# A state space layer inside a four-layer block: the fourth tap of its convolution moves to VectorE, the taps stay in SBUF, the diagonals are made over more turns, and the decays get a fourth slot

## The chip, the core and the metric

The kernel runs on one core of one Trainium2 chip. The metric is the device time of one execution in microseconds (us). Five engines work side by side, each through its own queue in order: TensorE (PE, with its weight loads PEld), VectorE (DVE), ScalarE (ACT), GpSimd (POOL) and SyncE (SP), which here issues almost all DMAs. An instruction that waits holds up all that stands behind it on its engine.

## What is computed

The input x holds 8 sequences of 512 positions with 256 channels. Three transformer layers come first; the change does not touch them. The fourth layer is a bidirectional state space (Mamba) layer with an MLP, conditioned by per-sequence scales and shifts. Its core, per direction:

```python
xz = h @ in_proj_W                       # 256 -> 1024
x, z = jnp.split(xz, 2, axis=-1)         # 512 channels each
xc = conv over time of x, 4 taps per channel, causal
x = silu(xc + conv_b)
xdbl = x @ x_proj_W                      # 512 -> 16 + 32 + 32
dt = softplus(xdbl[..., :16] @ dt_proj_W + dt_proj_b)
def step(hst, inp):                      # state: 512 channels x 32
    dA = exp(dt_t[:, :, None] * A)
    hst = hst * dA + dt_t[:, :, None] * B_t[:, None, :] * x_t[:, :, None]
    y = einsum('bdn,bn->bd', hst, C_t)
...
y = ys + Dp * x
return y * silu(z) @ out_proj_W
```

The forward and the backward direction are added, then `x + g1 * (fwd + bwd)`, a second norm and `silu(h @ w1) * (h @ w2) @ w3` follow. All is fp32.

## The kernel before, in words

**Shape of the fourth layer.** It takes the time from about 3455 us to the end. The work is 16 *passes*: for each of the 8 sequences b a forward pass, then a backward one (even numbers 0, 2, ... 14 are forward, odd ones backward). A pass (`recur`, L1145) is a loop of 64 *turns* k. A turn takes 32 channels with 8 of the 32 states each (128 partitions times two tiles of 512 positions). This text counts in *pairs* of turns, p = 0 to 31 in each pass, since the kernel issues them by twos. One pair is, on the engines:

- PE: 64 small matmuls that spread dt·B·x over the partitions into two PSUM tiles `bx` (`fill`, L1166). `bx` has three buffers, so the fill of a turn waits for the scans three turns back. The moving side of the fills are diagonal matrices `dg` made from B.
- ACT: four exponentials `da` (`decay`, L1179) into slots `da_t`, three of them, one for each turn in rotation: the decay of a turn waits for the scans three turns back. `da` is made from `dtr`, dt spread by DMA over the partitions (`spread`, L1110).
- DVE: four `tensor_tensor_scan` (L1190), one per tile, that run the recurrence; the output goes into one of four `hs` tiles (one for each pair). The order is scans of the first turn, then those of the second, and small DVE work is issued between the two.
- POOL: one product of the pair's `hs` with C (`cs`, L1194).

Every second pair PE adds up 8 matmuls over `hs` into `yc` (`sums`, L1222); they stand two pairs behind the POOL product that they read. Behind the last sum of a quarter pass (16 turns), `take` (L1203 on DVE backward, L1205 on ACT forward) moves `yc` to `ys`.

**The work around the recurrence** is issued between the turns by two Python generators, so the order on every queue is written out by hand (`manual_schedule`). At each even turn, after the pair's fills and decays, the main loop (L1313 to L1326) takes up to two pieces of each stream, `prep` and `post`, as long as a credit for PE work lasts. A piece says its cost by what it yields; a yield of LAST or more ends that stream's part of this turn.

- `prep` of the next pass (`before`, `prep3`): for a forward pass norm, `w_x0` product into `xp` (L950), convolution, SiLU of `u` (L959), products with `w_x` and `w_dt`, softplus, `uc` on POOL (L1006), transposes into `ut`. For a backward pass the same `xp` is convolved in the other direction (`convolve(b, True)`), and the gates `zs` are made (L912).
- `post` of the sequence before (`behind`): `project` (L1045) and `mlp3` (L1052).

All their products go through one PSUM tile `bank`, which has one buffer: the next product starts only after the last one was read. So backward passes carry the forward `prep` of the next sequence: norm at pairs 0 to 5, `xp` at pairs 6 and 7, convolution at pairs 8 to 13, SiLU at 14. Forward passes carry the backward convolution at pairs 0 to 3 and 8, `project` at 4 and 5, gates at 9 to 11 with SiLU, then both the projections of dt and the MLP.

**Convolution** (`convolve`, L916). Per group of 128 channels PE multiplies four diagonal tap matrices with four shifted views of `xp` (L929: four fp32 matmuls of 128x128 by 512, two records each in the trace), ACT adds the bias and writes `u` (L934), and SiLU follows later (L959). The 16 diagonal matrices are built once on DVE (L830), written to DRAM (`conv_s`) and read back in two halves before every convolution, through the ring `order` with `use` (L801) and `fetch` (L787), which has two buffers shared with `w_x0` and `w_z0`.

**Diagonals** (`diagonal`, L1124). For each of the four gp of the next pass there are four parts s: three on ACT (8 small activations each, L1133), one on POOL (L1137). They are due 1, 2, 3 and 4 turns after the fills of the last quarter have used the old ones (L1249).

**Decays of the next pass.** `spread` for the first `dtr` tile of the next pass is issued in turn 61, those for the next three at the head of the pass (L1151), behind the `cs` loads in SP's queue.

Of the kernel before, what the change touches and what calls it, by code (L numbers as in the profile page):

```python
# [25 lines left out]
N_U, N_UT, N_UC, N_DT, N_HS = 7, 5, 1, 5, 4  # L26
PAIRED = True
SUMS_LATE, DIAG, STAGGER, RATE, CREDIT = 3, "AAPA", 2, 4.0, 4.0
# [45 lines left out]
def dit_mamba_kernel(ctx: ExitStack, tc: tile.TileContext, t, out):  # L74
    nc = tc.nc
# [695 lines left out]
    with ExitStack() as mctx:  # L771
# [8 lines left out]

        conv_s = [scr.tile([128, 8, 128], F32, tag=f"cv{i}", name="conv_s", bufs=1) for i in range(2)]
        order = ["w_x0", "cv0", "cv1"]
        for b in range(B):
            order += ["cv0", "cv1", "w_z0"] + ["w_x0", "cv0", "cv1"] * (b + 1 < B)
        ring = {}

        def fetch(name, tag="wp", bufs=2):  # L787
            w = mp_.tile([128, 1024], F32, tag=tag, name="w", bufs=bufs)
            if name in ("w_x0", "w_z0"):
                src, k = t["w_in"].rearrange("(k p) m -> p k m", p=128), 2  # L790
                src = src[:, :, 0:D_IN] if name == "w_x0" else src[:, :, D_IN:]
            elif name[:2] == "cv":
                src, k = conv_s[int(name[2])], 8
            else:
                k = t[name].shape[0] // 128
                src = t[name].rearrange("(k p) m -> p k m", p=128)
            m = src.shape[-1]
            ring[name] = w[:, 0 : k * m].rearrange("p (k m) -> p k m", k=k)
            nc.sync.dma_start(ring[name], src)

        def use(name):  # L801

            assert order.pop(0) == name
            if order:
                fetch(order[0])
            return ring[name]

# [18 lines left out]

        for i in range(2):
            w = mp_.tile([128, 8, 128], F32, tag="wp", name="conv_d", bufs=2)
            for j in range(8):
                nc.vector.tensor_scalar(w[:, j, :], ident, vcol("convw", 8 * i + j), None, ALU.mult)  # L830
            nc.sync.dma_start(conv_s[i], w)
        dp_d = mp_.tile([128, 4, 128], F32, tag="dp_d", name="dp_d")
        for c in range(4):
            nc.vector.tensor_scalar(dp_d[:, c, :], ident, vcol("Dp", c), None, ALU.mult)

        da_t = [mp_.tile([128, 2, L], F32, tag=f"da{i}", name="da") for i in range(3)]
        xp = mp_.tile([128, 4, L + 6], F32, tag="xp", name="xp")
# [4 lines left out]

        WAIT, LAST = -1, 100
        st = {}
# [60 lines left out]
        def gates(b):  # L905
            h = st.pop(("hz", b))
            zs = mp_.tile([128, 4, L], F32, tag="zs", name="zs")
            st["zs", b] = zs
            w = use("w_z0")
            for c in range(4):  # L910
                p = yield from dense(w, h, 2, c)
                nc.scalar.copy(zs[:, c, :], p)  # L912
                taken()
                yield 2

        def convolve(b, rev):  # L916
            us = st["us"] = []
            for c in range(4):
                if c % 2 == 0:
                    w = use(f"cv{c // 2}")  # L920
                while n_u[0] - n_u[1] >= N_U:
                    yield WAIT
                n_u[0] += 1
                p = yield from free_bank()
                for k in range(4):
                    if k == 2:
                        yield 2
                    o = 6 - k if rev else k
                    nc.tensor.matmul(  # L929
                        p, w[:, (c % 2) * 4 + k, :], xp[:, c, o : o + L],  # L930
                        start=k == 0, stop=k == 3,
                    )
                us.append(mp_.tile([128, L], F32, tag="u", name="u", bufs=N_U))
                nc.scalar.activation(us[c], p, AF.Identity, bias=vcol("convb", c))  # L934
                taken()
                yield 2

        def prep3(b, rev):

            if not rev:  # L940
                h = st["hz", b]

                r = mp_.tile([128, L], F32, tag="uc", name="rstd", bufs=N_UC)
                yield from norm3(
                    h, h, xp[:, 0:2, 3 : L + 3], r, col(sc3[0], 0, b), col(sh3[0], 0, b)
                )
                w = use("w_x0")
                for c in range(4):
                    p = yield from dense(w, h, 2, c)
                    nc.scalar.copy(xp[:, c, 3 : L + 3], p)  # L950
                    taken()
                    yield 2
                yield from convolve(b, rev)
            us = st.pop("us")
            if rev:
                zs = st["zs", b]
                nc.scalar.activation(zs, zs, AF.Silu)
            for u in us:
                nc.scalar.activation(u, u, AF.Silu)  # L959
            use_exp_ln(pin=False)  # L960
            yield LAST
            p = yield from free_bank()
# [35 lines left out]
            use_exp_ln(pin=False)  # L998
            yield LAST
            nc.sync.dma_start(dt_s.rearrange("(c p) t -> p c t", p=128), dt)  # L1000
            st["dt", b, rev] = True

            def transposed(c):

                uc = mp_.tile([128, 4, 2, 64], F32, tag="uc", name="uc", bufs=N_UC)
                nc.gpsimd.tensor_tensor(uc, halves(us[c]), halves(dt[:, c, :]), ALU.mult)  # L1006
                yield 0
                yield 0
                while n_ut[0] - n_ut[1] >= N_UT:
# [41 lines left out]

        def mlp3(b):  # L1052
            x = st.pop(("x", b))
            fetch("w_g1", "wq", 1)
            h = mp_.tile([128, 2, L], F32, tag="h", name="h")
            g = mp_.tile([128, 3, L], F32, tag="g3", name="g3")
# [8 lines left out]
            use_exp_ln(pin=False)  # L1065
            yield LAST
            yield LAST
            for c in range(3):
                p = yield from dense(ring["w_g2"], h, 2, c)
                yield 2 + LAST  # L1070
                nc.vector.tensor_tensor(g[:, c, :], g[:, c, :], p, ALU.mult)
                taken()
            fetch("w_g3", "wq", 1)
            yield LAST
# [67 lines left out]

        n_pairs, done, projected, credit = [0], set(), set(), [0.0]

        def recur(step, nxt, ys):  # L1145
# [9 lines left out]

            hs, yc, bx, da_of = {}, {}, {}, {}

# [14 lines left out]

            def decay(k):
                c, gp, j = k // 16, k % 16 // 4, k % 4
                da = da_of[k] = da_t[n_pairs[0] % 3]
                n_pairs[0] += 1
                for i in range(2):
                    g = 2 * gp + i
                    nc.scalar.activation(  # L1179
                        da[:, i, :], dtr[step, 4 * c + j], AF.Exp, scale=negA[:, 4 * c + j, g : g + 1]  # L1180
                    )

            def scan(k):
                t_, j = divmod(k, 2)
                if j == 0:
                    hs[t_] = mp_.tile([128, 2, 2, L], F32, tag="hs", name="hs", bufs=N_HS)
                da, x = da_of.pop(k), bx.pop(k).rearrange("p r (t i) -> p i (r t)", i=2)
                for i in range(2):
# [10 lines left out]
            def take(c):  # L1199

                assert rev or b == 0 or b - 1 in projected
                if rev:
# [28 lines left out]
            for k in range(n_k):  # L1231
                c, gp, j = k // 16, k % 16 // 4, k % 4
                run_due(1)
                if PAIRED:
                    if k % 2 == 0:
                        fill(k)
                        fill(k + 1)
                        decay(k)
                        decay(k + 1)
                else:  # L1240
                    fill(k)
                    decay(k)
                n_ut[1] += k % 16 == 15
                later(2, lambda k=k: scan(k))
                if j == 3:
                    later(2 + SUMS_LATE, lambda c=c, gp=gp: sums(c, gp))
                    if c == 3 and nxt:
                        for s in range(4):
                            later(1 + s, lambda gp=gp, s=s: diagonal(nxt, gp, s))  # L1249
                        later(4, lambda gp=gp: spread_c(nxt, gp))  # L1250
                if c < 3:
                    if k % 16 in (6, 13, 14, 15):
                        spread(step, 4 * (c + 1) + (6, 13, 14, 15).index(k % 16))
                elif k % 16 == 13 and nxt and ("dt",) + nxt in st:
                    spread(nxt, 0)
                yield k
# [28 lines left out]
        def behind(b, ys):  # L1285
# [3 lines left out]
            yield from project(b, ys)  # L1289
            yield from mlp3(b)  # L1290
            if b + 1 < B:
# [13 lines left out]
        for i, step in enumerate(steps):  # L1305
# [7 lines left out]
            for k in recur(step, nxt, ys):  # L1313


                if k % 2 == 0 or not PAIRED:
                    credit[0] = min(credit[0] + (RATE if PAIRED else RATE / 2), CREDIT)
                    first = b and not rev and b - 1 not in projected
                    for stream in (post, prep) if first else (prep, post):
                        for _ in range(2):  # L1320
                            cost = next(stream, WAIT) if credit[0] > 0 else WAIT
# [3 lines left out]
                            if cost >= LAST:  # L1325
                                break  # L1326
            for _ in prep:
                pass
# [112 lines left out]
```

## Time and profile before

| quantity | value |
|---|---|
| median of 3 runs | 6533.63 us (6531.69 to 6535.91) |
| the profiled execution | 6532.14 us |
| its span, first to last instruction | 6530.3 us |
| first scan of the fourth layer | 3564.6 us |
| last scan ends | 6459.6 us |
| pass 0, pass 1 | 177.1, 175.9 us |
| forward passes 2 to 14 | 188.6 to 192.4 us |
| backward passes 3 to 13 | 176.3 to 178.5 us |
| pass 15, with nothing to prepare | 145.2 us |

Pass lengths are counted from the scans in the timeline, 128 to a pass, from first scan to first scan. In the profile a group is a line of the kernel with an engine, its busy time, the mean of one instruction, and the idle time of that engine ahead of it with what ended it. Two activations on ACT overlap a little, so four decays take 2.45 us although one shows 0.71; four scans on DVE take 4.47 us although one shows 1.20. The granted clock of PE was 0.96 of full speed on average.

### The profile page before, as it was taken

What the parts mean: (1) busy time and instruction counts of PE and PEld (TensorE: products, weight loads), DVE (VectorE), ACT (ScalarE), POOL (GpSimd) and SP (SyncE); (2) the same over time, 40 slices, a digit from 0 to 9 for tenths busy, and PEclk for the clock granted to TensorE, in tenths of its full rate; (3) what the DMA queues carried; (4) which work ended last, traced back from release to release, by engine and by line L of the source; (5) the groups of instructions that cost most, each with busy time, mean ns of one, the idle gap of its engine ahead of it and who ended that gap; (6) DMA issues with size and microseconds to landing.
All of it is one profiled execution on the core that took longest, in us unless ns stands there. A gap on an engine that the chain in (4) does not pass through costs nothing.

```text
span 6530.3 us, 200997 instructions
## 1 busy us (share of the span) xinstructions
PE 5907.6 (90%) x89056; PEld 2936.4 (45%) x89056; DVE 4073.5 (62%) x5042; ACT 3552.8 (54%) x6919; POOL 3664.6 (56%) x1464
## 2 busy tenths in 40 slices
PE   8999999999999989999986889888888889888887
PEld 4333345555555553333332444444444444444443
DVE  4555545454555445444521887878888887878886
ACT  2444444333343333444434776777777776777773
POOL 1010126565556662111101888888888888888896
PEclk8999999999999999999997999999999999999999
DMA  2101100100000000101002111222221212222120
GB/s 85 26 22 28 32 31 27 33 17 27 27 17 26 27 17 26 42 21 29 20 11 71 58 46 57 68 61 62 60 69 57 71 42 61 68 59 63 55 63 24
DMA packets 173457, 278.16 MB, mean 43 GB/s; under 512 B 40993, under 2 KB 58913, under 8 KB 172593
## 3 DMA queue, kind: packets, MB, share of 16 engines
q1 hardware_dynamic: 172048, 264.27, 13.8%
q8 instruction: 703, 11.52, 0.8%
q14 instruction: 162, 1.32, 0.1%
q10 hardware_dynamic: 544, 1.05, 0.0%
HBM read 203.30 MB, written 35.65 MB: 37 GB/s over the span
## 4 chain that ended last, share of the span: by engine, by line
PE 66%; POOL 12%; ACT 10%; issue 6%; DVE 4%; SPq 1%; DMA 1%; POOLq 0%; DVEq 0%; ACTq 0%
PE s L380 10%; PE s L673 8%; POOL hs L1194 8%; PE bx L1166 7%; PE s L636 5%; PE s L586 4%; PE bank L859 4%; PE yc L1222 4%; PE bank L929 4%; PE o L606 3%; PE s L497 3%; ACT da L1179 3%; PE o L537 3%; PE s L527 3%; DVE hs L1190 2%
## 5 line engine op out<-in xcount | busy, mean ns | idle before, releaser
L1190 DVE TENSOR_TENSOR_SCAN hs<-da,bx 128x512 f32<-128x512 f32 x2048 | 2310.2, 1199 | 542.1 <-ACT da L1179 347.9
L1194 POOL TENSOR_TENSOR hs<-hs,cs 128x2048 f32<-128x2048 f32 x512 | 2322.7, 4563 | 347.6 <-DVE hs L1190 242.1
L1179 ACT ACTIVATE da<-dtr,negA 128x512 f32<-128x512 f32 x2048 | 1342.9, 714 | 284.4 <-DVE hs L1190 246.4
L1166 PE MATMUL bx<-dg,ut 64*32 64x128 f32 x65536 | 1125.6, 276 | 252.3 <-DVE hs L1190 158.7
L1166 PEld LDWEIGHTS bx<-dg,ut 64*32 64x32 f32 x65536 | 940.8, 107 | 652.7 <-issue 469.2
L518 POOL TENSOR_SCALAR pr<-pr,sums 128x512 f32<-128x512 f32 x512 | 796.8, 1575 | 572.1 <-DVE sums L516 560.1
L591 DVE TENSOR_REDUCE negp<-s 128x1 f32<-128x512 f32 x1024 | 637.5, 683 | 586.3 <-PE s L586 586.0
L642 ACT ACTIVATE pt<-s 128x512 f32<-128x512 f32 x1024 | 528.0, 601 | 440.9 <-PE s L636 440.8
L1222 PE MATMUL yc<-hs,r 128*32 128x512 f32 x4096 | 614.8, 634 | 71.1 <-POOL hs L1194 70.9
L509 ACT ACTIVATE pr<-s,negm 128x512 f32<-128x512 f32 x512 | 345.1, 686 | 298.4 <-DVE negm L508 284.9
L528 DVE COPY pt<-s 128x512 f32<-128x512 f32 x512 | 322.0, 683 | 193.8 <-PE s L527 179.6
L508 DVE TENSOR_REDUCE negm<-s 128x1 f32<-128x512 f32 x512 | 317.3, 682 | 142.1 <-PE s L497 142.0
L586 PE MATMUL s<-kT,qT 32*128 32x512 f32 x2048 | 366.7, 651 | 35.9 <-ACT pt L642 18.2
L673 PE MATMUL s<-g,w_w 128*128 128x512 f32 x768 | 365.4, 623 | 23.9 <-ACT g L737 14.6
L1133 ACT ACTIVATE dg<-eye,bt 128x64 f32<-128x64 f32 x1536 | 381.5, 345 | 0.0
L352 POOL TENSOR_TENSOR xs<-x 128x512 f32<-128x512 f32 x48 | 61.0, 1271 | 566.1 <-DVE x L662 187.2
L380 PE MATMUL s<-h,w_w 128*128 128x512 f32 x768 | 364.1, 615 | 12.2 <-POOL h L371 12.2
L380 PE MATMUL s<-h,wqkv 128*128 128x512 f32 x768 | 365.9, 611 | 5.1 <-POOL h L371 5.1
L636 PE MATMUL s<-q,kT 32*128 32x512 f32 x2048 | 364.8, 647 | 2.4 <-DVE qs L453 1.9
L699 POOL COPY wide<-rec 128x1024 f32<-128x1024 f32 x16 | 16.6, 1037 | 622.3 <-DVE rec L697 622.3
L1222 PEld LDWEIGHTS yc<-hs,r 128*32 128x32 f32 x4096 | 126.3, 112 | 463.0 <-issue 292.1
L527 PE MATMUL s<-base,pr 128*128 128x128 f32 x2048 | 266.2, 281 | 43.0 <-POOL pr L518 38.5
(168 smaller groups left out, 6336.3 us busy)
## 6 DMA issues: line engine op xcount, KB each, us to landing
dtr<-dt_s SPq DMA_DIRECT2D x1024, 64.0 KB
cs<-c_s SPq DMA_DIRECT2D x256, 128.0 KB
wqkv<-in_wqkv_dram SPq DMA_DIRECT2D x48, 512.0 KB
w<-conv_s SPq DMA_DIRECT2D x32, 512.0 KB
dt_s<-dt SPq DMA_DIRECT2D x16, 1024.0 KB
x_mid<-x SPq DMA_DIRECT2D x24, 512.0 KB
x<-x_mid SPq DMA_DIRECT2D x24, 512.0 KB
w<-in_w_g_dram SPq DMA_DIRECT2D x24, 384.0 KB
```

Of the source, the lines that this page charges most:

```text
L380: nc.tensor.matmul(p, w[:, k, o : o + 128], src[:, k, :], start=k == 0, stop=k == n - 1)
L518: nc.gpsimd.tensor_scalar(p[:, j, :], p[:, j, :], sums[:, j : j + 1], None, ALU.mult)
L586: nc.tensor.matmul(ss[j], u.qT[r, c, qt * 128 : (qt + 1) * 128], u.kT[r, c, :], start=True, stop=True)
L591: nc.vector.tensor_reduce(negp[c % 2][:, qt, i : i + 1], ss[j], AX.X, ALU.max, negate=True)
L636: nc.tensor.matmul(ss[j], u.kT[r, c, i * 128 : (i + 1) * 128], q2[u, c][r, :], start=True, stop=True)
L642: nc.scalar.activation(pt[j // 2][:, j % 2, :], ss[j], AF.Exp)
L673: nc.tensor.matmul(p, w[:, first + c, m * 128 : (m + 1) * 128], srcs[c], start=c == 0, stop=c == n - 1)
L1166: nc.tensor.matmul(bx[k][32 * n : 32 * n + 32, r, 128 * s : 128 * s + 128], uts[c][64 * r : 64 * r + 64, s, 32 * j : 32 * j + 32], d[64 * ...
L1179: nc.scalar.activation(da[:, i, :], dtr[step, 4 * c + j], AF.Exp, scale=negA[:, 4 * c + j, g : g + 1])
L1190: nc.vector.tensor_tensor_scan(h, back(da[:, i, :]), back(x[:, i, :]), 0.0, ALU.mult, ALU.add)
L1194: nc.gpsimd.tensor_tensor(hs[t_], hs[t_], cs[step, k % 16 // 4][:, None, :, :].to_broadcast([128, 2, 2, L]), ALU.mult,)
L1222: nc.tensor.matmul(yc[c][32 * j : 32 * j + 32, :], r32, h[j // 2][:, j % 2, i, :], start=False, stop=gp == n_p - 1 and i == 1, tile_positi ...
```

## The change

- **Convolution.** PE does three taps. The fourth reads `xp` without a shift in both directions; DVE multiplies it with its weight and adds PSUM in one `scalar_tensor_tensor` that writes `u`. The activation with the bias on ACT goes; the bias moves into the SiLU. The piece ends its stream's part of the turn, so the DVE instruction is issued one even turn after its matmuls, between the two halves of that pair's scans on DVE.
- **Taps.** 12 diagonal matrices stay in SBUF. The trip through DRAM and the 32 loads go. The ring keeps `w_x0` and `w_z0` alone, with one buffer; the next is fetched after the last product that uses it (`used`).
- **Diagonals.** The four parts are due 1, 4, 7 and 10 turns after, in place of 1, 2, 3 and 4; the part on POOL moves by four turns.
- **Decays.** Four slots in place of three; `decay` moves out of `recur` unchanged (AHEAD is 0, so each pair's decays are issued where they were). The first four `dtr` tiles of the next pass are issued in turns 54, 61, 62 and 63.
- **MLP.** Its `h` takes the second half of `ys` in place of a tile of its own.
- **Turns.** After a change of ACT's table a piece yields ALONE, which also ends the turn for the other stream. The listing of the built program shows what this does in a forward pass: the square of the MLP's norm is issued at pair 8 in place of 11, behind the SiLU; the scale and shift of its `h` at pair 17 in place of 16, behind softplus; its six first matmuls at pairs 18 and 19 in place of 17 and 18.

```diff
-PAIRED = True
+N_DA, AHEAD, SPREAD = 4, 0, (6, 13, 14, 15)
...
-        conv_s = [scr.tile([128, 8, 128], F32, tag=f"cv{i}", name="conv_s", bufs=1) for i in range(2)]
-        order = ["w_x0", "cv0", "cv1"]
+        order = ["w_x0"]
         for b in range(B):
-            order += ["cv0", "cv1", "w_z0"] + ["w_x0", "cv0", "cv1"] * (b + 1 < B)
+            order += ["w_z0"] + ["w_x0"] * (b + 1 < B)
...
-        for i in range(2):
-            w = mp_.tile([128, 8, 128], F32, tag="wp", name="conv_d", bufs=2)
-            for j in range(8):
-                nc.vector.tensor_scalar(w[:, j, :], ident, vcol("convw", 8 * i + j), None, ALU.mult)
-            nc.sync.dma_start(conv_s[i], w)
+        conv_d = mp_.tile([128, 12, 128], F32, tag="conv_d", name="conv_d")
+        for c in range(4):
+            for k in range(3):
+                nc.vector.tensor_scalar(
+                    conv_d[:, 3 * c + k, :], ident, vcol("convw", 4 * c + k), None, ALU.mult
+                )
...
-        da_t = [mp_.tile([128, 2, L], F32, tag=f"da{i}", name="da") for i in range(3)]
+        da_t = [mp_.tile([128, 2, L], F32, tag=f"da{i}", name="da") for i in range(N_DA)]
...
-                for k in range(4):
+                for k in range(3):
                     if k == 2:
                         yield 2
                     o = 6 - k if rev else k
                     nc.tensor.matmul(
-                        p, w[:, (c % 2) * 4 + k, :], xp[:, c, o : o + L],
-                        start=k == 0, stop=k == 3,
+                        p, conv_d[:, 3 * c + k, :], xp[:, c, o : o + L],
+                        start=k == 0, stop=k == 2,
                     )
                 us.append(mp_.tile([128, L], F32, tag="u", name="u", bufs=N_U))
-                nc.scalar.activation(us[c], p, AF.Identity, bias=vcol("convb", c))
+                yield 1 + LAST
+
+                nc.vector.scalar_tensor_tensor(
+                    us[c], xp[:, c, 3 : L + 3], vcol("convw", 4 * c + 3), p, ALU.mult, ALU.add
+                )
                 taken()
-                yield 2
...
-            for u in us:
-                nc.scalar.activation(u, u, AF.Silu)
+            for c, u in enumerate(us):
+                nc.scalar.activation(u, u, AF.Silu, bias=vcol("convb", c))
             use_exp_ln(pin=False)
-            yield LAST
+            yield ALONE
...
-                            later(1 + s, lambda gp=gp, s=s: diagonal(nxt, gp, s))
+                            later(1 + 3 * s, lambda gp=gp, s=s: diagonal(nxt, gp, s))
...
-                if c < 3:
-                    if k % 16 in (6, 13, 14, 15):
-                        spread(step, 4 * (c + 1) + (6, 13, 14, 15).index(k % 16))
-                elif k % 16 == 13 and nxt and ("dt",) + nxt in st:
-                    spread(nxt, 0)
+                if k % 16 in SPREAD:
+                    i = SPREAD.index(k % 16)
+                    if c < 3:
+                        spread(step, 4 * (c + 1) + i)
+                    elif nxt and ("dt",) + nxt in st:
+                        spread(nxt, i)
...
-            yield from mlp3(b)
+            yield from mlp3(b, ys[:, 2:4, :])
...
+                        if cost >= ALONE:
+                            break
```

## The prediction

> **What bounds the kernel now.** I first read the page's shares and slices, for which stretch the change touches:
>
> ```profile
> PE 5907.6 (90%) x89056; PEld 2936.4 (45%) x89056; DVE 4073.5 (62%) x5042; ACT 3552.8 (54%) x6919; POOL 3664.6 (56%) x1464
> ...
> DVE  4555545454555445444521887878888887878886
> ACT  2444444333343333444434776777777776777773
> POOL 1010126565556662111101888888888888888896
> ```
>
> Up to slice 21 (about 3455 us) lie three layers that stay as they are. In the fourth, DVE, POOL and PE are all eight to nine tenths busy: no engine bounds all of it, so the stage decides. Next, the groups that make a pair of turns:
>
> ```profile
> L1190 DVE TENSOR_TENSOR_SCAN hs<-da,bx 128x512 f32<-128x512 f32 x2048 | 2310.2, 1199 | 542.1 <-ACT da L1179 347.9
> L1194 POOL TENSOR_TENSOR hs<-hs,cs 128x2048 f32<-128x2048 f32 x512 | 2322.7, 4563 | 347.6 <-DVE hs L1190 242.1
> L1166 PE MATMUL bx<-dg,ut 64*32 64x128 f32 x65536 | 1125.6, 276 | 252.3 <-DVE hs L1190 158.7
> ```
>
> A pair costs POOL 4.56, DVE 4.47 (from scan to scan where nothing waits), PE 1.96 for fills and half of 1.85 for sums. Pass 15, with nothing else to do, takes 145.2 = 32 x 4.54: POOL's pace. The others take 177 and 190, so some 32 and 45 us per pass are the work woven in. Third, busy time by stage, for backward pass 7 and forward pass 8 (columns: stretch, length, then PE, PEld, DVE, ACT, POOL busy, clock, DMA):
>
> ```profile
> 4847.05:4882.30 35.25, 29.16 (x850) 15.28 (x856) 32.63 (x29) 25.77 (x51) 35.25 (x10) 1.00 0.27 72
> ...
> 4891.78:4928.88 37.10, 34.85 (x872) 18.48 (x856) 27.69 (x26) 17.79 (x28) 25.92 (x7) 1.00 0.07 23
> 4928.88:4983.15 54.27, 47.87 (x1410) 26.15 (x1394) 45.67 (x41) 41.24 (x61) 45.15 (x13) 0.91 0.20 57
> 4983.15:5023.74 40.59, 31.19 (x1152) 18.66 (x1134) 36.48 (x33) 37.13 (x110) 40.59 (x13) 1.00 0.16 49
> 5023.74:5047.05 23.31, 23.31 (x575) 12.29 (x560) 19.05 (x18) 18.57 (x40) 22.44 (x7) 1.00 0.40 116
> ...
> 5172.00:5212.80 40.80, 35.80 (x1119) 20.19 (x1098) 36.76 (x34) 37.90 (x112) 40.80 (x13) 1.00 0.33 97
> ```
>
> Read each row's length against its fullest engine. Row 1 (backward, pairs 0 to 6) and the two last quarters (40.59, 40.80) are POOL's to the last digit: what frees ACT there frees nothing. The backward convolution stage (row 2: pairs 8 to 13) and the forward head (23.31: pairs 0 to 3, convolution again) are PE's. Last, the waits, 3750 to 6450 us (14.6 passes; total, times, longest):
>
> ```profile
> ACT da L1179 <- DVE hs L1190: 235.1, 388, 3.3
> DVE hs L1190 <- ACT da L1179: 232.3, 87, 6.9
> ...
> ACT u L934 <- PE bank L929: 160.7, 45, 5.4
> DVE hs L1190 <- PE bx L1166: 139.8, 92, 5.9
> ```
>
> The third row: ACT stands behind the convolution, with decays queued behind it.
>
> **Part by part.** Terms are in us, minus is a gain.
>
> *Fourth tap, backward (pairs 8 to 13).* PE loses four fp32 matmuls; in the timeline four in a row (eight records) take 3.70, 0.93 each: 34.85 - 3.7 = 31.1. DVE gets four instructions; the nearest row is the `scalar_tensor_tensor` of PSUM and SBUF at L1046, 0.75 long, next scan 0.67 later: 24 scans x 1.12 + 4 x 0.67 + 0.6 (`take`) = 30.2. ACT loses four activations of 0.69 and their waits. So 31 at best. One stretch of PE stays too long for three `bx` buffers: pair 11, with 2.8 of convolution, 1.9 of L1215 and L1217 and 1.85 of sums, 6.5 between two fills. DVE holds 3 x 2.24 = 6.7 in store, of which 1.96 go to the fills on either side, so some 1.8 of wait remain there (4.04 before). I take 33 for 37.1: **-4**.
>
> Does the tap wait? It is issued one even turn behind its matmuls and half a pair of scans into the next work; by the groups with their idle time, L1079, which reads three matmuls with the same yields, waited 3.0 in 14 (0.2 each), L1046 behind four matmuls 17.1 in 14 (1.2 each). I take 0.2, nearest in shape, inside the 33; the other end is 1.2 x 60 taps in the loop = 73. The `bank` is now freed by DVE; behind it on PE stand the next channel's taps and all later fills. The two fills of the next pair (1.96) cover that.
>
> *Forward head (pairs 0 to 3).* PE 23.31 less three matmuls = 20.5; DVE 16 x 1.12 + 3 x 0.67 + 0.6 = 20.5; the early `dtr` loads take a 1.96 wait off ACT, off the path if PE leads. 20.8: **-2.5**. *Fourth channel at pair 8*: one matmul of 0.93, on PE's path through the gates: **-1**.
>
> *SiLU burst, forward pair 11.* Ahead of the decays for pair 12 ACT runs table load 1.28, 1.91, 2.17, load 1.28, and the square 1.06; DVE then waited 6.50. The square goes to pair 8, where an activation of 0.69 has left: -1.05. SiLU with a bias vector: L934 with one shows 0.69, the plain copy from PSUM 0.59, so +0.1 x 4, overlapped +0.3, in both passes: forward **-0.75**, backward **+0.3**.
>
> *MLP one pair later (pairs 16 to 21).* Softplus' burst loses 1.52, so a wait of 2.79 at pair 18 goes; but at pair 19 the last first-MLP matmuls now stand behind the transposes, whose copy frees `bank`, and ACT's next burst (1.28 + 1.49 + 1.28) behind them, so the wait of 2.59 at pair 20 about doubles: **0**, -2.6 to +2.6.
>
> *Diagonals.* ACT's 24 activations per gp (0.24 each in a row) move apart: 10.6 per two pairs becomes some 9. But POOL needs 10.37 there (two products and a diagonal of 1.25), and is full. Only POOL's own diagonal counts: the last gp's slides into the next pass. Into a forward head (POOL idle 0.87) it leaves a POOL-bound quarter: **-1.25**; into a backward head it goes from one POOL-bound row to the next: 0.
>
> *Fourth decay slot.* At most one more half pair (2.24) for each of the 87 waits of DVE on `da`: -195. But ahead of the long bursts ACT waits for PE (copies of `bank`, L912, L994), and PE is held by three `bx`; in the last quarters POOL holds. I take 0; for the range a quarter, -50. It adds no wait, so no loss.
>
> *Taps in SBUF.* 32 loads of 512 KB leave an SP queue with DMA engines a quarter busy: 0. With one buffer the next `w_x0` or `w_z0` load waits on PE's last product with `dtr` loads behind it, which are due more than two turns later: 0; without that cover, waits like `da` on `dtr` before (30.3 in 21), 1.4 x 15 = +22. `h` in `ys`: `take` of pair 26 waits on matmuls of pair 23, long done: 0.
>
> *Start, once.* Four convolution groups in a chain of 3.72 + 0.70 become 2.8 + 0.75: -3.5; `hz` no longer follows 1 MB of `conv_s` out (landing in 5.67, where another 512 KB took 2.73): -1.5. *Pass 0*, forward without MLP, DVE near full at the convolution: -2.
>
> **Sum.** Per sequence -4 - 2.5 - 1 - 0.75 + 0.3 - 1.25 = -9.2; seven of them -64.4; with -5 and -2: -71 of 6532.1. The median stands 1.5 above that execution: **6462**.
>
> *A rule against it.* The Trainium skill, "Perfetto Trace Analysis", section "Optimizing Scalar/DVE Operations", says that of work which either engine can do some should go from a full DVE to Scalar; here it goes the other way. In the convolution stage DVE is 27.7 of 37.1 busy and ACT 17.8, so the row sides with the rule on load. What the row adds is that PE is fuller than both. By the rule alone, 60 x 0.67 = 40 would be lost.
>
> **Rivals.**
> 1. *POOL takes it back.* POOL is 40.6 and 35.3 full around these stages; if DVE only arrives earlier at a queue that POOL holds, the head's and the tail's terms (-2.5, -1.25) and half of the convolution's (-2) go: 7 x 5.75 = 40: **6502**. For: rows 1, 4 and 6. Against: POOL idles 11 in row 2 and 9 in the next, time to drain.
> 2. *More than counted.* DVE may lead POOL by up to 1.5 pairs (sums stand that far behind); in the POOL-bound quarters it leads by under one, as ACT was just as late (10.6 to 10.37). With ACT eased it enters both heads some 2 earlier: 15 x 2 + some slot gain = 45: **6417**.
> 3. *Slower: the tap holds DVE.* Place: each of 60 taps, between scans. If PE's lag puts the matmuls behind the fill that the waiting half pair hides, DVE idles, `bx` is freed late, and PE's fills follow late: a ring. Price up to a half pair of scans, 2.24 + 0.2: 60 x 2.24 = 134 against 71 gained: **6596**. It decides from 71/60 = 1.2 a tap, which is L1046's wait.
> 4. *No change*: gains are as long as the waits that they turn into: **6533**.
>
> **Chances.** Forecast (6435 to 6485) 0.50, rival 1 0.22, rival 2 0.14, rival 3 0.07, no change 0.07. Range 6410 (rival 2 and the slot's quarter) to 6515 (rival 1 with part of the tap's 73). A measurement tells 0.2% (13 us) from no change: faster 0.86, same 0.07, slower 0.07.
>
> **What would show it.** Backward pairs 8 to 13 near 33 and forward pairs 0 to 3 near 21, with few waits of DVE on `bank`; the last quarters still POOL's, backward about 39.3; pair 12 forward waiting 5.4. Wrong if taps wait over 1 us each, if POOL idles in the last quarters (slots did matter), or if pairs 16 to 21 lengthen.

## The result, and the profile after

The changed kernel takes **6473.75 us** (median of 4 runs, 6471.57 to 6475.56); the kernel before 6532.66 (4 runs, 6521.96 to 6535.91). The ratio is 0.9913, with a 95% interval of 0.9895 to 0.9930: faster by 59 us. The forecast was 6462. The profiled execution took 6473.94, with a span of 6472.1.

The page of the changed kernel, shares, slices and the three groups of a pair. Lines are renumbered: L1204 is the scan (L1190 before), L1208 the POOL product (L1194), L1190 the fill (L1166), L1165 the decay (L1179).

```profile
PE 5842.6 (90%) x88928; PEld 2917.0 (45%) x88928; DVE 4110.2 (64%) x5102; ACT 3513.7 (54%) x6855; POOL 3665.9 (57%) x1464
...
DVE  4554545544554544455531887888878888888886
...
POOL 1110126655556662111001888888989888988896
...
L1204 DVE TENSOR_TENSOR_SCAN hs<-da,bx 128x512 f32<-128x512 f32 x2048 | 2311.1, 1198 | 425.3 <-ACT da L1165 245.7
L1208 POOL TENSOR_TENSOR hs<-hs,cs 128x2048 f32<-128x2048 f32 x512 | 2323.7, 4564 | 278.1 <-DVE hs L1204 201.7
...
L1190 PE MATMUL bx<-dg,ut 64*32 64x128 f32 x65536 | 1123.4, 276 | 249.1 <-DVE hs L1204 154.3
```

PE lost 65 us of work, DVE gained 37, and yet DVE's idle time ahead of its scans fell from 542.1 to 425.3, by 117. Most of that is the taps, which now stand there (64 x 0.72 = 46), and the shorter span (58). Nothing got faster by itself: the scan's mean is 1198 ns (1199 before), the product's 4564 (4563).

The same stages as in the prediction, backward pass 7 and forward pass 8 of the changed kernel (stretch, length, then PE, PEld, DVE, ACT, POOL busy, clock, DMA): backward pairs 0 to 6, 8 to 13 and 24 to 31, forward pairs 0 to 3 and 24 to 31. Three rows of the prediction begin or end 0.2 to 1.2 us beside the scans. From first scan to first scan, as here, they are in the kernel before (backward pairs 0 to 6, forward pairs 0 to 3 and 24 to 31; the other two, 37.10 and 40.59, lie at the scans already):

```profile
4847.05:4883.49 36.44, 30.35 (x936) 16.47 (x941) 32.63 (x30) 26.96 (x53) 36.44 (x11) 1.00 0.26 70
5023.74:5046.80 23.06, 23.06 (x557) 12.04 (x541) 18.80 (x17) 18.32 (x40) 22.19 (x7) 1.00 0.40 118
5171.47:5212.84 41.37, 36.13 (x1122) 20.56 (x1130) 37.29 (x35) 38.35 (x112) 41.11 (x13) 1.00 0.32 95
```

The changed kernel:

```profile
4822.51:4860.34 37.83, 32.07 (x958) 18.55 (x965) 32.57 (x29) 30.13 (x69) 37.23 (x12) 0.95 0.13 40
4868.64:4899.99 31.35, 31.24 (x896) 17.08 (x877) 30.03 (x30) 20.77 (x30) 23.86 (x6) 1.00 0.10 28
...
4953.09:4992.92 39.83, 31.18 (x1119) 18.15 (x1104) 36.68 (x33) 32.81 (x94) 39.83 (x12) 1.00 0.17 56
4992.92:5015.12 22.20, 22.20 (x618) 12.18 (x600) 20.59 (x20) 20.58 (x53) 22.20 (x7) 1.00 0.18 52
...
5137.71:5179.39 41.68, 35.48 (x1164) 21.10 (x1166) 37.28 (x35) 33.08 (x94) 40.66 (x12) 1.00 0.31 98
```

The second row is the gain: 37.10 became 31.35, still PE's to within 0.1 (31.24), with DVE at 30.03 close behind. The backward last quarter is POOL's as before (39.83 of 39.83), though ACT fell from 37.1 to 32.8 there. The forward one is so nearly (40.66 of 41.68; 41.11 of 41.37 before). The first row, a backward head, became **longer**: 36.44 to 37.83, and in the other backward passes 36.2 to 36.7 became 37.4 to 39.0 (above all at pair 5 in four of the six, at pair 3 in pass 7 and at pair 6 in pass 11).

All the pairs, counted scan to scan and averaged over forward passes 2 to 14 and backward passes 3 to 13 (us per pass, minus is a gain; pairs left out moved little):

| forward | change | backward | change |
|---|---|---|---|
| pairs 0 to 4, convolution | -2.2 | pair 5 | **+1.8** |
| pairs 8 and 9, fourth channel | -0.8 | pairs 8 to 13, convolution | **-5.0** |
| pair 11, SiLU | -0.55 | pair 14 | -1.3 |
| pair 13 | -0.5 | pair 15 | +1.0 |
| pairs 16 to 21, MLP | **+2.05** | pair 17 | -0.9 |
| all 32 | -2.6 | pair 29, last quarter | -1.6 |
| | | all 32 | -5.4 |

How far a pair moves by chance can be read from e2, e3, e4 and e9 below: where their edits have no part, pair averages differ from the changed kernel's by up to 0.5, but forward pair 15 by up to 0.8 and forward pair 21 by up to 1.6. So the -0.5 of forward pair 13 says little.

Added up: 7 x -2.6, 6 x -5.4, pass 0 -7.0, pass 1 +1.0, pass 15 +0.2: -56 between the first scan and the last. The start and the tail bring the span to -58.

The waits of the changed kernel, 3750 to 6390 us (total, times, longest):

```profile
ACT da L1165 <- DVE hs L1204: 232.8, 386, 2.0
DVE hs L1204 <- ACT da L1165: 180.9, 59, 6.2
...
ACT ut L1023 <- PE bank L1019: 145.7, 47, 4.8
...
DVE hs L1204 <- PE bx L1190: 127.6, 76, 7.3
...
POOL uc L1011 <- ACT dt L1002: 30.8, 9, 4.7
...
DVE u L937 <- PE bank L930: 13.1, 16, 1.3
```

One line of the kernel before, over the same window, to be laid beside the one of `ut`:

```profile
ACT ut L1018 <- PE bank L1014: 59.4, 47, 2.3
```

The line of `u L937` is rival 3's whole case: 56 taps in this stretch waited 13.1 in all, 0.23 each, the longest 1.3. ACT's wait on the convolution (160.7 before) is gone, yet ACT did not wait less for PE: its groups of 20 us and more that wait for `bank` add up to 463.9 before and to 476.6 after, `ut` alone 59.4 and 145.7. ACT's wait for a late PE moved to other products. The list alone doesn't say what that wait had cost; e5 and e12 part it from PE's work.

### The profile page after: what moved, and what is told of

Read it like the earlier page. It is cut to its first block, busy times and chain, and to the rows that moved or that the text cites. A ratio compares the mean times of both kernels' runs of the same rounds, so it can differ in the third digit from the quotient of the medians.

```text
span 6472.1 us, 200572 instructions
## 1 busy us (share of the span) xinstructions
PE 5842.6 (90%) x88928; PEld 2917.0 (45%) x88928; DVE 4110.2 (64%) x5102; ACT 3513.7 (54%) x6855; POOL 3665.9 (57%) x1464
## 3 DMA queue, kind: packets, MB, share of 16 engines
q1 hardware_dynamic: 167152, 246.44, 12.5%
q14 instruction: 161, 1.32, 0.1%
## 4 chain that ended last, share of the span: by engine, by line
PE 68%; ACT 10%; POOL 9%; DVE 6%; issue 5%; DMA 1%; SPq 1%; POOLq 0%; DVEq 0%; ACTq 0%
PE s L381 10%; PE s L674 8%; PE bx L1190 8%; POOL hs L1208 5%; PE bank L861 5%; PE s L637 5%; PE s L587 5%; PE yc L1236 5%; DVE hs L1204 4%; PE o L607 3%; PE s L498 3%; PE o L538 3%; ACT da L1165 3%; PE s L528 3%; PE bank L930 3%
## 5 line engine op out<-in xcount | busy, mean ns | idle before, releaser
L1204 DVE TENSOR_TENSOR_SCAN hs<-da,bx 128x512 f32<-128x512 f32 x2048 | 2311.1, 1198 | 425.3 <-ACT da L1165 245.7
L1208 POOL TENSOR_TENSOR hs<-hs,cs 128x2048 f32<-128x2048 f32 x512 | 2323.7, 4564 | 278.1 <-DVE hs L1204 201.7
L1165 ACT ACTIVATE da<-dtr,negA 128x512 f32<-128x512 f32 x2048 | 1335.4, 713 | 260.6 <-DVE hs L1204 247.9
L1190 PE MATMUL bx<-dg,ut 64*32 64x128 f32 x65536 | 1123.4, 276 | 249.1 <-DVE hs L1204 154.3
L1190 PEld LDWEIGHTS bx<-dg,ut 64*32 64x32 f32 x65536 | 941.8, 107 | 655.9 <-issue 473.9
```

What stands on the lines that cost most here:

```text
L1165: nc.scalar.activation(da[:, i, :], dtr[step, 4 * c + j], AF.Exp, scale=negA[:, 4 * c + j, g : g + 1])
L1190: nc.tensor.matmul(bx[k][32 * n : 32 * n + 32, r, 128 * s : 128 * s + 128], uts[c][64 * r : 64 * r + 64, s, 32 * j : 32 * j + 32], d[64 * ...
L1204: nc.vector.tensor_tensor_scan(h, back(da[:, i, :]), back(x[:, i, :]), 0.0, ALU.mult, ALU.add)
L1208: nc.gpsimd.tensor_tensor(hs[t_], hs[t_], cs[step, k % 16 // 4][:, None, :, :].to_broadcast([128, 2, 2, L]), ALU.mult,)
```

## The experiments

Each kernel is the changed one with the edit shown, except where another base is named. The kernel before took 6534.0, 6532.78, 6535.97 and 6529.79 us beside the four groups (1 to 4, 5 to 8, 9 to 11, 12); the ratios are to it.

| run | median us | ratio, 95% interval |
|---|---|---|
| the change | 6473.75 | 0.9913, 0.9895 to 0.9930 |
| e1 all taps on PE, old place | 6532.75 | 0.9995, 0.9986 to 1.0005 |
| e2 three slots | 6475.90 | 0.9906, 0.9886 to 0.9926 |
| e3 diagonals close | 6470.29 | 0.9899, 0.9884 to 0.9914 |
| e4 POOL's part early | 6470.55 | 0.9901, 0.9883 to 0.9918 |
| e5 PE still four | 6518.51 | 0.9977, 0.9966 to 0.9987 |
| e6 softplus LAST | 6467.45 | 0.9896, 0.9881 to 0.9911 |
| e7 tap alone | 6484.20 | 0.9923, 0.9906 to 0.9940 |
| e8 no ALONE | 6485.82 | 0.9925, 0.9911 to 0.9940 |
| e9 part by pass | 6459.46 | 0.9882, 0.9864 to 0.9900 |
| e10 both | 6442.84 | 0.9854, 0.9835 to 0.9873 |
| e11 tap left out | 6467.93 | 0.9899, 0.9882 to 0.9916 |
| e12 bias on ACT, one turn on | 6514.19 | 0.9979, 0.9969 to 0.9988 |

**Theory and rivals.** The theory: the gain is the convolution's, since PE's stretch got shorter. The rivals: ACT was relieved (its activations and their wait are gone); the order of the work changed; the other edits did it.

### e1: all four taps on PE

```diff
-        conv_d = mp_.tile([128, 12, 128], F32, ...)
+        conv_d = mp_.tile([128, 16, 128], F32, ...)
...
-                for k in range(3):
+                for k in range(4):
...
-                yield 1 + LAST
-                nc.vector.scalar_tensor_tensor(us[c], xp[...], vcol("convw", 4 * c + 3), p, ...)
+                nc.scalar.activation(us[c], p, AF.Identity, bias=vcol("convb", c))
                 taken()
+                yield 2
...
```

The bias leaves the SiLU again.

> The changed kernel with all four taps on TensorE again (16 diagonals in SBUF), the bias activation on ScalarE again; all else as changed. Theory (the gain is PE's shorter convolution): the backward convolution stage, pairs 8 to 13, goes from 31.5 us back to about 36.5, the forward head by 1 to 2, some 40 us in all: 6505 to 6520. Rival (the gain is the diagonals, the slots and the early loads, the tap only moves work): 6470 to 6485.

Measured 6532.75: nothing is left of the gain, where the theory had expected 6505 to 6520. So without the tap the other edits are worth nothing together. (With the tap in place one of them, ALONE, is worth some 8 to 12, as e8 shows below: the edits depend on each other, and their shares do not simply add up.) But this edit moves three things, PE's work, the engine of the reader of `bank`, and its place in the order; e5 and e12 part them.

### e2: three slots

`N_DA = 3`.

> The changed kernel with three slots of decays. Theory (ahead of ACT's bursts PE holds, not the slots): 6474 to 6480, all pairs within 0.3 us. Rival (each of the 59 remaining waits of DVE on the decays would grow by up to half a pair, 2.24): 6500 to 6570.

It took 6475.90, in the theory's range. Nearly every pair is within 0.5, the largest difference is -0.8 at forward pair 21, the pair that scatters most. The fourth slot does nothing here that can be seen. The 180.9 that DVE still waits for decays is not for want of a slot.

### e3 and e4: when the diagonals are due

`later(1 + s, ...)` in e3; `later(3 if DIAG[s] == "P" else 1 + 3 * s, ...)` in e4, which moves only POOL's part back.

> The changed kernel with the diagonals due 1, 2, 3, 4 turns after, as before. Theory (the last quarters are POOL's; what moves the time is POOL's own diagonal): backward last quarter 41.2 in place of 39.8, backward pair 5 back from 6.5 to about 4.5, net within 6 us of the changed kernel: 6468 to 6480. Rival (ACT was the bound there): last quarters longer by 1 to 2 us in every pass, 6490 to 6505.

> The changed kernel with only POOL's part of the diagonals due after 3 turns again, ScalarE's parts spread as changed. Theory: the new wait at backward pair 5 (sums wait for POOL, which has the moved diagonal and the norm's product ahead) goes, about 2 us in each of 7 passes; the backward last quarter grows by 1.2: 6462 to 6474. Rival (the wait at pair 5 has another cause, the loads or the single ring buffer): pair 5 stays at 6.5 to 9.6, time 6474 to 6484.

They took 6470.29 and 6470.55, both in the theory's range, and both a little under the change, which the intervals do not resolve. Both take 1.70 off backward pair 5 and put 1.3 and 1.2 onto backward pair 29. Since e4 leaves ACT's parts spread out and gives the same, the new wait at pair 5 is POOL's one moved instruction. At the head of a pass POOL made one diagonal before, and makes two now: the last gp's, which stood in the head already, comes later, and the third gp's has slid in. POOL's timeline in the kernel before, at the head of backward pass 7 (start, length, what it does):

```profile
4851.96 1.29 POOL L1137 TENSOR_TENSOR dg<-eye,bt 128x512 f32<-128x512 f32 x1
4853.14 13.67 POOL L1194 TENSOR_TENSOR hs<-hs,cs 128x2048 f32<-128x2048 f32 x3
4866.73 2.43 POOL L895 TENSOR_TENSOR hz<-hz,rstd 128x1024 f32<-128x1024 f32 x1
```

And in the changed kernel at the head of backward pass 3, behind its first diagonal:

```profile
4106.02 9.08 POOL L1208 TENSOR_TENSOR hs<-hs,cs 128x2048 f32<-128x2048 f32 x2 [0.95 <-DMA cs<-c_s]
4115.06 1.22 POOL L1142 TENSOR_TENSOR dg<-eye,bt 128x512 f32<-128x512 f32 x1
4116.23 4.58 POOL L1208 TENSOR_TENSOR hs<-hs,cs 128x2048 f32<-128x2048 f32 x1
4120.76 2.38 POOL L897 TENSOR_TENSOR hz<-hz,rstd 128x1024 f32<-128x1024 f32 x1
4123.10 13.53 POOL L1208 TENSOR_TENSOR hs<-hs,cs 128x2048 f32<-128x2048 f32 x3
```

POOL has no gap from 4106.02 on, and the second diagonal (1.22) and the norm's product (2.38) now lie on either side of one of the pairs' products. PE's sums then waited 2.56 for POOL, the fills stand behind the sums, and the scan waited 2.93 for its `bx`.

### e5: PE still does four

```diff
-                    conv_d[:, 3 * c + k, :], ident, vcol("convw", 4 * c + k), None, ALU.mult
+                    conv_d[:, 3 * c + k, :], ident, vcol("convw", 4 * c + k), 1.0 if k else 0.5,
+                    ALU.mult, ALU.mult,
...
-                for k in range(3):
-                    if k == 2:
+                for i, k in enumerate((0, 0, 1, 2)):
+                    if i == 3:
...
```

> The changed kernel with one edit: PE still does four matmuls for each group of the convolution. The first tap's diagonal is halved and used twice, so the output stays the same; the fourth tap stays on DVE, the bias stays in the SiLU, and the order of all work is that of the changed kernel. Theory (the gain is PE's shorter work in the two convolution stages): backward pairs 8 to 14 lose most of the 5 to 6.5 us that they had gained per pass and the forward head its 1 to 2.5; time 6510 to 6530 us. Rival (the gain is ACT's: the activations with the bias, which waited for PE with decays queued behind them, are gone): the pairs stay within 0.5 of the changed kernel's and the time is 6474 to 6490 us. In between, both have a part: each us above 6474 is PE's, out of 59.

It took 6518.51, in the theory's range: 45 of the 59 (42 by the ratios) go with nothing but PE's fourth matmul. Backward pairs 8 to 13 and forward pairs 0 to 3 of the same passes:

```profile
4888.96:4923.20 34.24, 34.24 (x890) 18.43 (x874) 30.46 (x29) 21.04 (x30) 23.82 (x6) 1.00 0.10 26
5018.20:5043.46 25.26, 25.15 (x624) 13.42 (x606) 20.70 (x21) 20.85 (x54) 22.56 (x7) 1.00 0.18 46
```

Both are PE's to the last tenth, with DVE and POOL where the change had them: 34.24 against 31.35, 25.26 against 22.20, some 3 for the four and the three matmuls of 0.93 taken away. ACT is as relieved as in the change (21.04 and 20.85 busy, 20.77 and 20.58 there), and most of the gain is gone all the same.

### e12: the bias on ACT, at the tap's place

As e1, but with `yield 1 + LAST` kept ahead of the activation, so that the order is the changed kernel's.

> The changed kernel with all four taps on PE again, from 16 matrices in SBUF, and the bias on ACT again, but the activation issued where the changed kernel has DVE's tap, one even turn behind its matmuls, so that the order of all work is the changed kernel's. PE's work is that of the run e5_pe_four_still (6518.5 us); against e1_tap_on_pe (6532.75 us) only the place of the activation, and with it the order of the streams, differs. Theory (the 14 us that PE's shorter work does not explain are the place: an activation that waits no more holds up no decays): 6512 to 6524 us. Rival (they are the engine: ACT's 60 activations take time from decays wherever they stand): 6528 to 6540 us.

It took 6514.19, in the theory's range, beside e5's 6518.51 with overlapping intervals: with the same work on PE and the same place, no difference between ACT and DVE as the reader of the bank is seen. (One thing more differs: e5 issues three matmuls and then one, e12 two and two.) Against e1 only the place differs, and the streams' order with it; that is worth 18 us by the medians and 10 by the ratios, whose intervals just overlap. The wait of ACT on the convolution, first in e1 and then in e12, over 3750 to 6390 us:

```profile
ACT u L935 <- PE bank L930: 214.3, 56, 7.9
```

```profile
ACT u L936 <- PE bank L930: 100.4, 45, 4.6
```

Issued one turn later, it waits half as long, and backward pairs 8 to 14 of e12 are 3.7 shorter than those of e1 (-2.9 at pair 9), of which pairs 5 and 15 take back 2.3. How much of the 18 us is the place and how much the other order of the forward stream (pairs 13 and 14: +3.2, -4.8) is not parted here, and no run has three taps on PE with the reader in the old place.

### e11: the tap left out

The fourth tap is left out of the convolution; in the place of the DVE instruction stands `nc.scalar.copy(us[c], p)`.

> The changed kernel without the fourth tap: it is left out of the convolution, and in its place, at the same point of the order, ACT copies the bank to u. PE's work and order are those of the changed kernel. Theory (of the 59 us about 45 are PE's shorter work and the other 14 ACT's activations with their waits): ACT's copies come back without the wait, as their matmuls lie one even turn back, and DVE is rid of 60 taps; the time is 6468 to 6485 us. If DVE's taps cost what they last (60 times 0.7 = 42 us), it is 6432 to 6450 us; if ACT's share is the queueing itself, it is 6485 to 6500 us.

It took 6467.93, at the lower edge of the theory's range and with an interval that overlaps the change's: 64 taps of 0.72 on DVE and 64 copies of 0.59 on ACT cost the same here. The taps cost no 42 us more than the copies; what either costs against nothing at all is not shown.

### e7 and e8: the tap alone, and ALONE

e7 is the kernel before with the tap on DVE (the new `convolve` with taps still read through DRAM, and the bias in the SiLU). e8 is the changed kernel with ALONE equal to LAST.

> The kernel before with the fourth tap on DVE and the bias in the SiLU, and nothing else of the change: the taps still come through DRAM, three slots of decays, the diagonals due 1 to 4 turns after, no ALONE. Theory (the tap carries the whole gain): 6465 to 6485 us. Rival (the tap needs another edit with it: without ALONE the MLP's norm runs earlier in the forward pass, beside the SiLU, and may take back what the convolution gives): 6490 to 6520 us.

> The changed kernel with ALONE made equal to LAST: a piece that changes ACT's table ends only its own stream's part of the turn, as in the kernel before; all else as changed. Theory (ALONE costs the 2 us at pairs 16 to 21 of a forward pass and gives little elsewhere): 6450 to 6470 us. Rival (ALONE keeps the MLP's activations from between two tables, so without it ACT holds up decays): 6485 to 6520 us, with longer waits of DVE on ACT in forward pairs 8 to 17.

They took 6484.20 and 6485.82, the same to within their intervals: e7 as its theory expected, e8 outside its theory's range and in its rival's. So e8, which has taps in SBUF, one ring buffer, four slots, later diagonals and `h` in `ys`, has in sum nothing over e7, which has none of these. ALONE is worth what lies between e8 and the change: 12 us by the medians, 8 by the ratios, with intervals that overlap, so the size is rough. Two lines of e8's waits, to be laid beside 180.9 and 30.8 of the change:

```profile
DVE hs L1204 <- ACT da L1165: 218.7, 79, 7.5
...
POOL uc L1011 <- ACT dt L1002: 89.8, 14, 8.9
```

Without ALONE the MLP's activations stand among the SiLU and softplus, and DVE waits longer for decays and POOL longer for dt (forward pairs 15 to 17: +10.4, pairs 13 and 18: -8.9).

### e6: softplus without ALONE

`yield LAST` behind softplus; ALONE stays behind the SiLU.

> The changed kernel with one word changed: after softplus the piece yields LAST in place of ALONE, so the scale and shift of the MLP's h are issued at pair 16 of a forward pass again and its first matmuls at pairs 17 and 18, as in the kernel before. Theory (the shift by one pair costs about 2 us per forward pass: pairs 16 and 17 gain 2.8, pairs 18 and 19 lose 5.5): the loss at pairs 18 and 19 goes, the gain at 16 and 17 too, and the time is 6456 to 6468 us. Rival (what is lost there is only moved from one place of the pass to another): 6470 to 6480 us.

It took 6467.45, 6 less and in the theory's range. The intervals do not resolve this from the change; the pairs do: 18 and 19 shorten by 5.5, 16 and 17 lengthen by 3.2, and a forward pass is 1.2 shorter. Beside e8, which has ALONE in neither place (0.9925, 0.9911 to 0.9940), ALONE behind the SiLU is worth 18 us by the medians, with intervals that touch. So ALONE pays behind the SiLU and not behind softplus.

### e9 and e10: a version that takes both

```diff
-                            later(1 + 3 * s, ...)
+                            later(3 if DIAG[s] == "P" and not rev else 1 + 3 * s, ...)
```

> The changed kernel with POOL's part of the diagonals due 3 turns after the fills when the next pass is a backward one, and 7 turns after, as in the changed kernel, when it is a forward one. Theory (the late part costs 1.7 us at pair 5 of each backward pass that begins with it, and saves 1.2 us in the last quarter of each backward pass): both gains are kept, 7 or 8 times 1.7, so 6459 to 6466 us. Rival (the pass that follows takes up most of what the head gives back, as it did when the part was early in all passes, which gave 3 us): 6468 to 6474 us.

> The run e9_part_by_pass with LAST in place of ALONE after softplus as well. Theory (the two places do not touch each other, so the gains add: about 6 us less than e9_part_by_pass): 6452 to 6462 us. Rival (one hides the other): 6462 to 6468 us.

e9: **6459.46**, in the theory's range; its interval just overlaps the change's. POOL's timeline at the head of its backward pass 3:

```profile
4098.86 1.23 POOL L1142 TENSOR_TENSOR dg<-eye,bt 128x512 f32<-128x512 f32 x1
4100.11 13.61 POOL L1208 TENSOR_TENSOR hs<-hs,cs 128x2048 f32<-128x2048 f32 x3
4113.68 2.38 POOL L897 TENSOR_TENSOR hz<-hz,rstd 128x1024 f32<-128x1024 f32 x1
```

The diagonal is done ahead of the head's products; three of them run in a row, and the norm's product comes a pair later. Pair 5 loses 1.63, pair 29 keeps its gain (+0.01). e10: **6442.84**, the fastest, 90 us under the kernel before. Its runs lie far apart (6431.59 to 6456.69), the interval overlaps e9's, and it is lower than the theory's 6452 to 6462. In the profiled executions, from the first scan of the fourth layer to the last, the change takes 2838.6, e6 10.0 less, e9 9.1 less and e10 23.0 less. So there the two gains nearly add, as the theory had it (the profiled execution of e10 took 6456.69), and much of the rest may be the scatter of the runs.

## Why the prediction was right, and where not

Forecast 6462 by a sum of -71; measured -59, in the forecast case (6435 to 6485). That the number came so near is in part luck, for errors of both signs lie in it. Against the forecast terms the forward passes are 11 short in all, pass 1 is 6 short, and the start with the tail 3; pass 0 gave 5 more and the other backward passes 3 more. By its own steps:

- **Fourth tap, backward, -4: right, a little small.** -5.0 in pairs 8 to 13; the -1.3 in pair 14 is nearly taken back by pair 15 (+1.0), where the SiLU with its bias (+0.3 by the forecast) is not parted from it. PE's 31.1 and DVE's 30.2 were 31.24 and 30.03 in pass 7. The 33 was too careful: the wait kept for pair 12 was 1.32 in that row, and little else was left to wait. DVE's timeline there, the tap between two halves of a pair:

```profile
4886.14 0.72 DVE L937 SCALAR_TENSOR_TENSOR u<-xp,vec,bank 128x512 f32<-128x512 f32 x1
4886.78 2.32 DVE L1204 TENSOR_TENSOR_SCAN hs<-da,bx 128x512 f32<-128x512 f32 x2
4890.41 6.78 DVE L1204 TENSOR_TENSOR_SCAN hs<-da,bx 128x512 f32<-128x512 f32 x6 [1.32 <-PE bx L1190]
```

- **The reason behind it: PE, right.** e5 gives some three quarters of the 59 to PE's matmul, and between e5 and e12 the engine of the reader makes no difference that is seen. What the prediction did not name is the place: it counted the later turn only as a possible cost to the tap (0.2, measured 0.23), and not as a gain to the stage (10 to 18 by e1 and e12, with the order that goes with it).
- **Forward head, -2.5: right in sum.** -1.0 in pairs 0 to 3 and -1.3 in pair 4. PE was not 20.5 but 22.20 of 22.20: it used part of the time for fills of later pairs (`bx` fills have 564 records there, 499 in the like stretch before), so part of the gain came out one pair later. (POOL is full in that row too, but e4, which takes its diagonal out of the forward head, leaves pairs 0 to 4 within 0.1.)
- **Fourth channel -1, SiLU -0.75: right** (-0.8, -0.55).
- **MLP 0, bounds -2.6 to +2.6: +2.05, near the upper bound.** Both halves came as described: pairs 16 and 17 -2.8, pairs 18 and 19 +5.5. The doubled wait was the larger one, which e6 shows by taking it away. By the prediction's own words it was wrong here: "if pairs 16 to 21 lengthen" was one of its signs. Over seven forward passes this is 14 us.
- **Diagonals: half wrong, and beside the MLP the step that cost most.** The backward last quarter's -1.25 was measured as -1.3 (-1.6 at pair 29, +0.3 in the pairs about it). But "into a backward head it goes from one POOL-bound row to the next: 0" was false: the forward last quarter, which the diagonal left, became shorter by only 0.2, and the backward head, which it entered, became longer by 1.8 at pair 5 and 2.1 in all. The prediction's row for that quarter begins half a us late; from its first scan the quarter is 41.37 long with POOL at 41.11, not POOL's to the last digit. And it was not the last gp's diagonal that slid into the next pass, since that one stood there already, but the third gp's. At the head the products stand ahead of sums, sums ahead of fills, and the norm's 2.38 falls into the same two pairs. By what e4 takes off again (1.7 in six passes, 3.5 in pass 1) the loss at the heads comes to some 14 us. e9 undoes this one term and lands at 6459.46; that it meets the 6462, which was forecast with the term at 0, is partly chance, since the MLP's 14 are still in it.
- **Fourth slot 0: right** (e2). **Taps in SBUF, one buffer, `h` in `ys` 0: right in sum** (e8 against e7, with the slots and the later diagonals in the same sum; e2 and e3 put those near 0).
- **Start -5: -3.** The four groups of the convolution went from 3.72 + 0.70 to 2.86 + 0.76, -3.2; the -1.5 of `hz` did not come (landing 5.48 for 5.67). That -3 and -3.2 agree is chance: of the four products into `xp` three took 3.8 in place of one (2.0 for the others), while the SiLU's table load left the chain and the first product behind it took 3.65 for 5.09. In the span the -3 does not show, since the first three layers, which the change leaves alone, ended 3.3 later in this execution.
- **Pass 0, -2: -7.0.** Pairs 5 and 17 gave 1.7 and 2.6, and their cause stays open; the last quarter gave 2.2. Pass 1 pays at its pair 5 (9.55 for 4.44). With POOL's diagonal back in its old place (e4) the last quarter is 1.2 longer again and that pair 3.5 shorter.

Rival 1 (POOL takes it back) named the right engine and the wrong stage: POOL took some 2 per backward pass at the head, not the convolution's gain. Rival 2's lead of DVE over POOL is not seen: the slots give nothing. Rival 3 was to decide at 1.2 a tap; the taps waited 0.23.

On the Trainium skill's advice ("Perfetto Trace Analysis", section "Optimizing Scalar/DVE Operations": where DVE is saturated, giving work that either can do to Scalar "may make sense"): e5 and e12 have it on DVE and on ACT with PE's work alike, at 0.9977 and 0.9979. Here the choice between the two is worth nothing that is seen, and the 40 us that the rule alone would have lost were not lost. In this stage DVE was 75% busy, and PE was the full engine.

## What to carry to other kernels

Read which engine fills each stage, and take work off that one, even onto an engine that is well filled itself: DVE at 75% of a PE-bound stage took four instructions for a gain of 5 us per backward pass. A wait that vanishes from the list is not the gain; keep the disputed work and change only its owner (e5, e12, e11) to see which part pays. When an instruction leaves a full engine's stage, look at the queue that it joins, by pass and by pair; here the same move was a gain before one kind of pass and a loss before the other, and doing it for one kind alone gave 14 us by the medians, whose intervals just overlap, and 9 between the first and the last scan of the profiled executions.

## What was not expected of the hardware

- A `scalar_tensor_tensor` of PSUM and SBUF, 128x512, between scans took 0.72 and delayed the next scan by 0.64 (4886.14 to 4886.78); 64 of them cost no more that could be measured than 64 copies on ACT in their place (e11), in a layer whose DVE is eight tenths busy.
- The GpSimd product kept its mean of 4564 ns (4563 before) beside 64 more DVE instructions.
- 18 MB less through the DMA queue (264.27 to 246.44 MB) and 32 loads of 512 KB fewer changed nothing that the runs tell: e8 without them and e7 with them take the same time, though other edits lie between the two as well.
